# Two graph layers in one kernel: O^T of a batch moved to the end of a step, directly ahead of the next scores, and the sums of x1 blocks moved behind

## The chip, the cores and the metric

The kernel runs on one core of a Trainium2 chip. Its time is the device time of one execution in microseconds (us). Before the change three runs took 2452.73, 2454.88 and 2456.25 us, so the median is 2454.88 us. One more execution was recorded by the hardware profiler; its span is 2452.6 us, and every row of a profile below comes from such a profiled execution.

The engines are named as the profile names them: PE (TensorE, matrix products; PEld is its loading of weights), DVE (VectorE), ACT (ScalarE), POOL (GpSimd) and SP (the queue that issues most transfers).

## The reference, cut to what matters

The input is 128 batches of 128 tokens with 512 features, and a 128x128 adjacency matrix for each batch. Two layers follow each other, each with a residual and a layer norm:

```python
# layer 0: attention with 8 heads of 64 features
q, k, v = x @ Wq + bq, x @ Wk + bk, x @ Wv + bv
attn = softmax(where(adj > 0, q @ k.T / 8, -1e9))      # for each head
x1 = layernorm(x + relu((attn @ v) @ Wo + bo))
# layer 1: graph attention
Wh = x1 @ W
e = where(adj > 0, leaky(Wh @ a1 + (Wh @ a2).T), -9e15)
out = layernorm(x1 + leaky(softmax(e, axis=1) @ Wh))
```

All of it is in fp32. O^T is the transposed output of attention of one batch, (attn @ v)^T, 512 features by 128 tokens, and x1 is the output of layer 0.

## The kernel before, in words

The work is a software pipeline over the batches. One pass of the loop `for t in range(-3, END)` (line 929, END = 124) is called a step. The order of every engine's instructions is the order in which the code records them (`manual_schedule`, line 855), so where a line stands in a step is where it stands in each engine's queue. In a step t from 3 on, the following is under way at once:

- the softmax of batch t (class Softmax): `scores` (L506) on PE, mask and maxima on DVE (L520, L529), `exp` and `divide` on ACT (L540, L554), with the reciprocals on DVE (L550) between them; then `spread`, which writes the probabilities to DRAM and fetches them back in blocks (L560, L566);
- the end of attention of batch t - 1 (the variable `last`): `transpose` of the probabilities into paT on DVE (L575), `attend`, which computes O^T on PE (L588), and `copy`, which moves O^T with its bias from PSUM to the tile oT on ACT (L602);
- the projections q, k and v of the next group of four batches (`group_product`, L354), a product at a time wherever `group()` stands;
- the product of a pair of batches (`pair_product`, L435), a product at a time wherever `pair()` stands: layer 0's with Wo (class LayerZero) in odd steps, layer 1's with W (class LayerOne) in even steps;
- layer 1's attention of batch t - 7 (class Edge): `turn` on PE (L784, L785), `product` on PE (L818) with a copy to the tile z on ACT (L824), and its norm a step later (the variable `fin`): L828, L829 and L632 on DVE, L638 and L640 on POOL, L653 on DVE.

The large products use the Strassen-Winograd scheme: seven products of half-size blocks in place of eight, called p1 to p7, in the order of the table ORDER (line 272): p1, p5, p6, p2, p7, p4, p3. They need sums of blocks of the left operand, which POOL computes: xS from xT (sum_x), oS from oT (Softmax.sum) and x1S from x1T (LayerZero.sum), each with the four operations of `left_blocks` (L263 to L266). Inside one scheme, p1, p6, p7 and p4 add up in one PSUM bank, p_y; between them ACT copies out what the bank holds (t0, t2 and t3; L446 for a pair), and the next product into p_y waits for that copy.

Scores and O^T use TensorE in parts. For the scores each matmul contracts over 64 rows, and the two heads of a couple use the upper and the lower half of the array's rows (the profile writes 64*128). For O^T each matmul has 64 output columns, and the two heads use the left and right halves of the columns (128*64). All other products use the whole array (128*128).

PSUM tiles of one bank come from a ring of five (`ps_mm`, line 97): scores, p_y, p_w, p_x, p_e, p_oT and p_h take their turn in it in the order in which the code asks for them. The group's products have three banks of their own (st_y, st_w, st_x).

Before the change, in a step from t = 3 on, O^T of batch t - 1 stands after `sm.divide(6, 7)` and `mask_float`, between the fifth product of the pair (p7) and the fourth `group()` of the step. Its copy follows at once in even steps; in odd steps it stands after `pair(2)`. In even steps the sums oS of the pair that is then complete follow the copy. The sums x1S of layer 0's pair stand at the end of an even step, after the transposes of x1T (L233). In steps with t % 4 == 0, `sum_x` gives POOL the sums of a whole group after `fin.rstd`; they work on twice as many elements.

The step ends with `fin.product` (p_h) and `fin.copy`, and the next one begins with the scores. After the loop, the rest of the work is written out as a list of pieces (PLAN, line 1142).

Of the kernel before, what the change touches and what calls it, by code (L numbers as in the profile page):

```python
# [24 lines left out]
def kernel(  # L25
# [95 lines left out]
    def load_blocks(w, columns, queue, spread_rows=True, only=None):  # L121

        for o, t in enumerate(columns):
            if only not in (None, o):
                continue
            if spread_rows:
                rows = w.rearrange("(q k c i) (o f) -> o q i k c f", q=4, k=2, c=2, o=2)
                for q in range(4):
                    queue.dma_start(t[32 * q : 32 * q + 32, :, :, :HALF], rows[o, q])
            else:  # L130
                rows = w.rearrange("(k c p) (o f) -> o k p c f", k=2, c=2, o=2)
                for k in range(2):
                    queue.dma_start(t[:, k, :, :HALF], rows[o, k])
# [4 lines left out]
    def right_blocks(t):  # L138

        return [  # L140
            lambda: nc.vector.tensor_sub(t[2], t[2], t[0]),
            lambda: nc.vector.tensor_sub(t[5], t[3], t[2]),
            lambda: nc.vector.tensor_sub(t[4], t[5], t[0]),
            lambda: nc.vector.tensor_sub(t[6], t[1], t[5]),
        ]

    def places(w):
        return [w[:, n] for n in range(7)]

    def columns(w):  # L150
        return w[:, 0:2], w[:, 2:4]
# [23 lines left out]
    def load_bias():  # L175
        nc.sync.dma_start(bo_b, bo.partition_broadcast(P))
        return [lambda: nc.vector.tensor_sub(bo_b[:, HALF:], bo_b[:, HALF:], bo_b[:, :HALF])]

    def load_w1():

        load_blocks(W1, columns(w1), nc.sync)
        a_b = work.tile([P, 2, D], F32, name="a_b", tag="x1T")
        nc.sync.dma_start(
            a_b.rearrange("p s f -> p (s f)"),
            a1.rearrange("f o -> (f o)").partition_broadcast(P),
        )
        sums = small.tile([P, 2, 2, 2, 2], F32, name="wa", bufs=1)

        def dots(k, o, c):
            def run():  # L190
                for s in range(2):
                    scr = work.tile([P, HALF], F32, name="wa_scr", tag="x1S")
                    nc.vector.scalar_tensor_tensor(
                        scr,
                        w1[:, 2 * o + k, c, :HALF],
                        1.0,
                        a_b[:, s, o * HALF : (o + 1) * HALF],
                        op0=ALU.mult,
                        op1=ALU.mult,
                        accum_out=sums[:, s, k, o, c : c + 1],  # L200
                    )

            return run

        def last_column(k, o):
            def run():
                for c in range(2):
                    nc.vector.tensor_add(
                        w1[:, 2 * o + k, c, HALF:],
                        sums[:, o, k, 0, c : c + 1],  # L210
                        sums[:, o, k, 1, c : c + 1],
                    )

            return run

        every = [(k, o) for k in range(2) for o in range(2)]
        ops = [dots(k, o, c) for k, o in every for c in range(2)]
        return ops + [last_column(k, o) for k, o in every] + right_blocks(places(w1))
# [19 lines left out]
    def load_x(b):  # L238
        X[b] = spread(x[b])

    def load_residual(b):

        X1[b] = work.tile([P, D], F32, name="x1", bufs=7)
        nc.sync.dma_start(X1[b], x[b])
# [7 lines left out]
    def sum_x(g):  # L252
        sums = big.tile([P, 3, 2, 2 * P], F32, name="xS")
        XS[g], ops = left_blocks(XT[g], sums)
        return lambda: [op() for op in ops]
# [219 lines left out]
    def load_mask(b):  # L475
        MF[b] = small.tile([P, P], I32, name="adj", bufs=2)
        nc.sync.dma_start(MF[b], adj[b])

    def mask_float(b):
        a = MF[b]  # L480
        MF[b] = small.tile([P, P], BF16, name="mf", bufs=9)
        nc.scalar.copy(MF[b], a)
# [362 lines left out]
    def on(b):  # L845
        return 0 <= b < B
# [14 lines left out]
    none = Nothing()  # L861
    group_steps = []
    later = []
    zero = {}
    chores = []
    sm = fin = edge = none
# [61 lines left out]
    END = B - GROUP  # L928
    for t in range(-3, END):
        pair_steps = []  # L930
        if t % GROUP == 1 and on(t + 3):
            group_steps, v_pieces, fetch_v = products((t + 3) // GROUP)
        if t % 2 == 1 and on(t - 3):
            pair_steps = zero[(t - 3) // 2] = LayerZero((t - 3) // 2)
            pair_steps = pair_steps.steps()
        if t % 2 == 0 and on(t - 6):
            pair_steps = LayerOne((t - 6) // 2).steps()

        def group(n=1):
            for _ in range(min(n, len(group_steps))):  # L940
                group_steps.pop(0)()
            for _ in range(min(3 * n if t == -3 else n, len(chores))):
                chores.pop(0)()

        def pair(n=1):
            for _ in range(min(n, len(pair_steps))):
                pair_steps.pop(0)()

        if on(t + 1):
            load_mask(t + 1)  # L950
        if t == -1:
            load_blocks(Wo, columns(wo), nc.sync, spread_rows=False)
            late_chores = right_blocks(places(wo)) + load_bias()
        if t == 1:
            late_chores = load_w1()
        if t in (0, 2):
            chores += late_chores

        last, sm = sm, Softmax(t) if on(t) else none
        sm.scores()  # L960
        if t % 2 == 1 and on(t - 3):
            zero[(t - 3) // 2].by()
            zero[(t - 3) // 2].bw()
        while later:
            later.pop(0).go_back()
        if t < 3:
            sm.maxima()
            group(2)
            if on(t - 2):
                load_residual(t - 2)  # L970
            if t == 0 and on(GROUP):
                sum_x(1)()
            sm.exp(0, 1, 2, 3)
            last.transpose()
            group()
            sm.reciprocals(0)
            sm.exp(4, 5, 6, 7)
            sm.reciprocals(1)
            sm.divide(0, 1, 2)
            group()  # L980
            last.attend()
            sm.divide(3, 4)
            last.copy()
            if t % 2 == 0 and t > 0:
                last.sum(0, 1, 2, 3)
            sm.divide(5, 6, 7)
            if on(t + 1):
                mask_float(t + 1)
        else:
            sm.maxima()  # L990
            group()
            edge = Edge(t - 7) if on(t - 7) else none
            edge.turn()
            edge.add()
            fin.residual()
            if on(t - 2):
                load_residual(t - 2)
            edge.maxima()
            fin.stats()
            fin.rstd()  # L1000
            if t % GROUP == 0 and on(t + GROUP):
                sum_x(t // GROUP + 1)()
            pair()
            sm.exp(0, 1, 2, 3)
            edge.exp()
            pair()
            sm.exp(4, 5)
            last.transpose()
            group()
            sm.reciprocals(0)  # L1010
            pair()
            sm.exp(6)
            fin.apply()
            fin.store()
            sm.exp(7)
            edge.divide()
            pair()
            sm.reciprocals(1)
            sm.divide(0, 1, 2, 3)
            group()  # L1020
            sm.divide(4, 5)
            pair()
            sm.divide(6, 7)
            if on(t + 1):
                mask_float(t + 1)
            last.attend()
            if t % 2 == 0:
                last.copy()
                last.sum(0, 1, 2, 3)
            group()  # L1030
        sm.spread()
        for b in x_turns(t):
            transpose_x(b)
        for b in x_turns(t + 1):
            load_x(b)
        if on(t + 1):
            mask(t + 1)
        pair(2)
        if t % 2 == 1 and t >= 3:
            last.copy()  # L1040
        if t % 2 == 0 and on(t - 4):
            layer = zero.pop((t - 4) // 2)
            layer.transpose(0)
            layer.transpose(1)
            layer.sum(0, 1, 2, 3)
        group(21 if t % GROUP == 0 else 1)
        fin = edge
        fin.product()
        fin.copy()

# [180 lines left out]
```

## Time and profile before

| what | value |
|---|---|
| median of three runs | 2454.88 us |
| span of the profiled execution | 2452.6 us |
| one step, from one scores block to the next (1016.01 to 1034.28 us) | 18.27 us |
| O^T on PE (L588), 2016 matmuls | 138.8 us busy, mean 280 ns of one |
| scores on PE (L506), 2048 matmuls | 148.8 us busy, mean 285 ns of one |
| ACT idle ahead of the copies of O^T (L602) | 192.0 us |
| POOL, one sum of x1 blocks (L263 to L266) | 726 to 742 ns |
| DVE, z's norm applied (L653), mean of 116 | 696 ns |

Busy time counts an engine as busy while any of its instructions runs; the matmuls of a block overlap, so their mean duration is longer than their share of the busy time. In the chain of waits each piece has its start, the time that it adds to the chain, and what it is. In the timeline each row has the start, the duration of the merged instructions from the first start to the last end, and in brackets the idle time before them and what ended it.

### The profile page before, as it was taken

The page shows a single profiled execution, that of the slowest core. Times are in us where ns is not written, and L with a number is a line of the kernel's source. Part 1 is how long each engine was busy: PE and PEld are TensorE (multiplying, and loading weights), DVE is VectorE, ACT ScalarE, POOL GpSimd, SP SyncE. Part 2 cuts the span into 40 slices and gives each one's busy share as a digit, 9 for nine tenths or more (in the row PEclk, how much of TensorE's full clock was granted, in tenths as well). Part 3 has the DMA queues.
Part 4 walks back from the last instruction along what each step waited for, and adds up shares of the span by engine and source line. Part 5 has one row for each costly group of instructions (what it writes and reads, how often), then busy time and mean ns, then how long its engine had stood idle before and what let it go on. Part 6 is the DMA issues. An engine that isn't in the chain of part 4 may idle for free.

```text
span 2452.6 us, 43635 instructions
## 1 busy us (share of the span) xinstructions
PE 2412.3 (98%) x13585; PEld 1989.0 (81%) x13585; DVE 1802.0 (73%) x3731; ACT 1478.2 (60%) x5334; POOL 789.8 (32%) x1195
## 2 busy tenths in 40 slices
PE   8899999999999999999999999999999999999997
PEld 6688888888888888888888888888888888888874
DVE  5667777777777777777777777777777777777777
ACT  3566556556656665665666566656656665666574
POOL 2222323323233223233233332232332333322325
PEclk9999999999999999999999999999999999999999
DMA  6644544544545445445445454454454454544443
GB/s 190 179 148 142 166 149 152 169 146 148 167 147 166 154 141 168 145 154 169 149 146 171 146 163 157 140 168 146 152 171 146 146 171 145 164 152 149 149 157 105
DMA packets 351111, 379.91 MB, mean 155 GB/s; under 512 B 38936, under 2 KB 255008, under 8 KB 350880
## 3 DMA queue, kind: packets, MB, share of 16 engines
q1 hardware_dynamic: 350016, 376.07, 47.7%
q8 instruction: 109, 1.79, 0.3%
q10 hardware_dynamic: 864, 1.05, 0.2%
q14 instruction: 122, 1.00, 0.1%
HBM read 240.91 MB, written 136.05 MB: 154 GB/s over the span
## 4 chain that ended last, share of the span: by engine, by line
PE 93%; issue 1%; DMA 1%; DVE 1%; ACT 1%; POOL 1%; SPq 1%; DVEq 0%; POOLq 0%; ACTq 0%
PE st_y L354 27%; PE p_y L435 17%; PE st_w L354 14%; PE p_w L435 9%; PE st_x L354 7%; PE lg L506 5%; PE p_oT L588 5%; PE p_x L435 4%; PE p_h L818 4%; PE p_e L784 1%; DMA wv_n<-wv 0%; SPq L228 0%; ACT pa L540 0%; POOL rstd L640 0%; PE p_e L785 0%
## 5 line engine op out<-in xcount | busy, mean ns | idle before, releaser
L638 POOL TENSOR_SCALAR ve<-mv 128x1 f32<-128x1 f32 x256 | 69.1, 270 | 1323.7 <-DVE mv L634 1316.3
L540 ACT ACTIVATE pa<-pa,nmax 128x128 f32<-128x128 f32 x1008 | 392.4, 392 | 37.2 <-DVE nmax L529 32.7
L554 ACT ACTIVATE pa<-pa,rs 128x128 f32<-128x128 f32 x1008 | 331.5, 395 | 30.2 <-DVE rs L550 30.2
L602 ACT ACTIVATE oT<-p_oT,b_cols 128x128 f32<-128x128 f32 x504 | 142.9, 366 | 192.0 <-PE p_w L435 189.4
L520 DVE TENSOR_TENSOR pa<-lg,mf 128x512 f32<-128x512 f32 x252 | 161.8, 684 | 101.7 <-PE lg L506 96.5
L331 ACT COPY st_t<-st_y 128x512 f32<-128x512 f32 x192 | 110.5, 575 | 156.2 <-PE st_y L354 156.2
L506 PEld LDWEIGHTS lg<-kT,qT 64*128 64x128 f32 x2048 | 124.2, 187 | 92.3 <-issue 92.3
L540 ACT ACTIVATION_READ_ACCUMULATOR pa<-pa,nmax 128x1 f32 x1008 | 190.6, 189 | 0.0
L640 POOL TENSOR_TENSOR rstd<-ve,mhalf 128x1 f32<-128x1 f32 x256 | 176.2, 688 | 21.3
L446 ACT COPY pr_t<-p_y 128x257 f32<-128x257 f32 (+1 forms) x375 | 137.1, 366 | 59.9 <-PE p_y L435 59.8
L575 DVE STREAM_TRANSPOSE paT<-paz 128x1024 f32<-128x1024 f32 x126 | 156.9, 1245 | 3.6 <-DMA paz<-pa_dram 1.8
L529 DVE TENSOR_REDUCE nmax<-pa 128x8 f32<-128x1024 f32 x126 | 153.7, 1220 | 4.4
L506 PE MATMUL lg<-kT,qT 64*128 64x128 f32 x2048 | 148.8, 285 | 0.0
L588 PEld LDWEIGHTS p_oT<-paT,v 128*64 128x64 f32 x2016 | 108.2, 137 | 46.8 <-issue 39.9
L588 PE MATMUL p_oT<-paT,v 128*64 128x128 f32 x2016 | 138.8, 280 | 5.0 <-DVE paT L575 5.0
L335 ACT ACTIVATE st_t<-st_y,b_cols 128x256 f32<-128x256 f32 x192 | 80.6, 470 | 97.2 <-PE st_y L354 97.2
L759 DVE TENSOR_TENSOR wh<-p_w,pr_t 128x257 f32<-128x257 f32 x122 | 51.5, 423 | 112.4 <-PE p_w L435 65.4
L435 PE MATMUL p_y<-w,x1T 128*128 128x257 f32 x496 | 131.6, 388 | 1.6 <-ACT wk L446 1.5
L435 PE MATMUL p_y<-wo,oT 128*128 128x256 f32 x504 | 132.7, 386 | 0.2 <-ACT p_y L456 0.2
L435 PE MATMUL p_y<-wo,oS 128*128 128x256 f32 x504 | 129.4, 379 | 0.0
L354 PE MATMUL st_y<-wv_n,xS 128*128 128x256 f32 x512 | 124.1, 385 | 4.0 <-ACT pa L554 2.3
L435 PE MATMUL p_y<-w,x1S 128*128 128x257 f32 x496 | 128.0, 380 | 0.0
(200 smaller groups left out, 5926.3 us busy)
## 6 DMA issues: line engine op xcount, KB each, us to landing
pa_dram<-pa SPq DMA_DIRECT2D x126, 512.0 KB, 2.6
paz<-pa_dram SPq DMA_DIRECT2D x504, 128.0 KB, 2.6
wv_n<-wv SPq DMA_DIRECT2D x224, 256.0 KB, 2.9
x<-in_x_dram SPq DMA_DIRECT2D x128, 256.0 KB, 2.9
x_dram<-x SPq DMA_DIRECT2D x128, 256.0 KB, 2.1
xz<-x_dram SPq DMA_DIRECT2D x512, 64.0 KB, 2.0
xz<-in_x_dram SPq DMA_DIRECT2D x496, 64.0 KB, 2.1
out_dram<-z SPq DMA_DIRECT2D x120, 256.0 KB, 2.5
```

Of the source, the lines that this page charges most:

```text
L354: nc.tensor.matmul(p[:, m, :], lhs, rhs, start=start and m == 0 and kc == 0, stop=True, skip_group_check=True,)
L435: nc.tensor.matmul(p[:, :width], xs()[n][:, kc, :], w[:, PLACE[n], kc, :], start=start and kc == 0, stop=True, skip_group_check=True,)
L446: nc.scalar.copy(t[:, :width], p[:, :width])
L506: nc.tensor.matmul(self.lg[r][:, c, :], q[rows, c, cols], k[rows, c, cols], start=c == 0, stop=True, skip_group_check=True,)
L520: nc.vector.tensor_add(by_head[:, r * NC : (r + 1) * NC], self.lg[r].rearrange("p c (b k) -> p c b k", b=4), mf.unsqueeze(1).to_broadcast( ...
L529: nc.vector.tensor_reduce(self.nmax, by_head, AX.XY, ALU.max, negate=True)
L540: nc.scalar.activation(self.pa[:, :, h, :], self.pa[:, :, h, :], AF.Exp, bias=self.nmax[:, h : h + 1], accum_out=self.sums[:, h : h + 1],)
L554: nc.scalar.activation(self.pa[:, :, h, :], self.pa[:, :, h, :], AF.Copy, scale=self.rs[:, h : h + 1])
L575: nc.vector.transpose(self.paT.rearrange("p h (a i) -> p a h i", i=32), self.paz.rearrange("p a (h k) -> p a h k", k=32),)
L588: nc.tensor.matmul(self.oT[r * HD : (r + 1) * HD, c, :], v[:, h * HD : (h + 1) * HD], self.paT[:, r * NC + c, :], start=c == 0, stop=True, ...
L602: nc.scalar.activation(OT[pair][:, c, h * P : (h + 1) * P], self.oT[:, c, :], AF.Identity, bias=b_cols[:, 1, c : c + 1],)
L640: nc.gpsimd.tensor_tensor(self.r, ve, mhalf, ALU.pow)
```

## The change

O^T of batch t - 1 (`last.attend`) leaves its place in the middle of the step and goes to the end, after `fin.product` and `fin.copy`, so that the next instructions on PE are the scores of the next step. Its copy on ACT and the sums oS on POOL go with it. The sums of x1 blocks are no longer recorded at the end of an even step; they are kept in a list and recorded in the next step, after `fin.rstd`. This holds from t = 3 on; earlier steps and PLAN are as they were.

```diff
--- before.py
+++ after.py
@@ -861,6 +861,12 @@
     none = Nothing()
     group_steps = []
     later = []
+    sums = []
+
+    def x1_sums():
+        while sums:
+            sums.pop().sum(0, 1, 2, 3)
+
     zero = {}
     chores = []
     sm = fin = edge = none
@@ -998,6 +1004,7 @@
             edge.maxima()
             fin.stats()
             fin.rstd()
+            x1_sums()
             if t % GROUP == 0 and on(t + GROUP):
                 sum_x(t // GROUP + 1)()
             pair()
@@ -1023,10 +1030,6 @@
             sm.divide(6, 7)
             if on(t + 1):
                 mask_float(t + 1)
-            last.attend()
-            if t % 2 == 0:
-                last.copy()
-                last.sum(0, 1, 2, 3)
             group()
         sm.spread()
         for b in x_turns(t):
@@ -1036,17 +1039,23 @@
         if on(t + 1):
             mask(t + 1)
         pair(2)
-        if t % 2 == 1 and t >= 3:
-            last.copy()
         if t % 2 == 0 and on(t - 4):
             layer = zero.pop((t - 4) // 2)
             layer.transpose(0)
             layer.transpose(1)
-            layer.sum(0, 1, 2, 3)
+            sums.append(layer)
         group(21 if t % GROUP == 0 else 1)
         fin = edge
         fin.product()
         fin.copy()
+        if t >= 3:
+
+            last.attend()
+            last.copy()
+            if t % 2 == 0:
+                last.sum(0, 1, 2, 3)
+        if t == END - 1 or t < 3:
+            x1_sums()
 
 
 
```

## The prediction

> **What bounds the kernel now.** I read the page's busy table and slices first, then busy time by stretch, then the chain of waits inside one step, then the timeline.
>
> ```profile
> PE 2412.3 (98%) x13585; PEld 1989.0 (81%) x13585; DVE 1802.0 (73%) x3731; ACT 1478.2 (60%) x5334; POOL 789.8 (32%) x1195
> ...
> 130.00:200.00 70.00, 70.00 (x406) 58.47 (x405) 48.08 (x94) 41.01 (x153) 22.52 (x32) 1.00 0.50 155
> 200.00:1200.00 1000.00, 1000.00 (x5666) 828.10 (x5665) 741.05 (x1540) 611.47 (x2221) 318.97 (x478) 1.00 0.48 155
> 1200.00:2340.00 1140.00, 1139.60 (x6457) 943.41 (x6456) 843.38 (x1747) 695.58 (x2527) 367.64 (x548) 1.00 0.47 154
> ```
>
> The columns of the last three are the stretch, its length, then the busy time of PE, PEld, DVE, ACT, POOL. From 130 to 2340 us PE is idle for 0.4 us in all, at full clock. No other engine sets the time there: only shorter PE work or a new PE wait moves it. So I price the PE sequence. The chain over one even and one odd step's seam (start, length, what):
>
> ```profile
> 1024.43 1.73 PE st_y L354 x8
> 1026.16 0.86 PE p_y L435 x4
> 1027.02 1.02 PE p_oT L588 x16
> 1028.04 1.93 PE st_x L354 x8
> 1029.97 0.86 PE p_y L435 x4
> 1030.83 0.86 PE p_w L435 x4
> 1031.69 1.73 PE st_y L354 x8
> 1033.42 0.86 PE p_h L818 x2
> 1034.28 1.09 PE lg L506 x16
> 1035.37 1.92 PE st_y L354 x8
> ```
>
> Eight 128x256 matmuls take 1.73 us, but 1.92 or 1.93 when they follow an O^T block (p_oT) or a scores block (lg). Each visit to a tiled block therefore leaves 0.19 us with the full-size work after it: O^T costs 1.02 + 0.19 = 1.21, scores 1.09 + 0.19 = 1.28. (The weight loads' waits in "issue" ahead of lg and p_oT, 92.3 and 40.6 us, are the same seams seen from PEld.)
>
> **What the Trainium skill says.** "TensorEngine Tiling (Array Packing)", Tiling Modes, Key Properties: changing the tiling mode, not just the tile, drains TensorE. The trace agrees as far as it can: a fixed price at each seam. It gives no price, and doesn't say whether a change between two tiled modes costs as much as one from full size. "Advanced Engine Details and Errata", VectorE Performance Modes, Mode Summary: VectorE's second SBUF port is shared with GpSimd, so two-port Vector instructions and GpSimd instructions block each other. The trace agrees: L653 on z takes 0.51 us alone and 1.25 us beside POOL's xS sums, in the third listing.
>
> **Part 1: O^T directly ahead of the scores.** Per step, before: full, O^T, full, scores, full. After: full, O^T, scores, full, for t = 3 to 122 (the O^T of t = 123 is followed by a full product): 120 pairs. Same instructions, one pass through full size less. Is the seam between two tiled blocks as cheap as one seam? The trace has one such pair, in the tail, in the other order (scores, then O^T):
>
> ```profile
> 2365.72 1.03 PE L435 MATMUL p_y<-w,wq 128*128 128x257 f32 x4
> 2366.68 1.16 PE L506 MATMUL lg<-kT,qT 64*128 64x128 f32 x16
> 2367.78 1.09 PE L588 MATMUL p_oT<-paT,v 128*64 128x128 f32 x16
> 2368.80 0.32 PE L784 MATMUL p_e<-ident,wh 128*128 128x128 f32 x1
> ```
>
> From start to start: scores to O^T 1.10, as 1034.28 to 1035.37 above; O^T to the next 1.02. So O^T put beside scores cost 1.02 there, not 1.21: 0.19 saved. I take the same for the reverse order, an estimate from these rows. Ends: nothing saved (if the seam between the two modes costs as much as the pass through full size), or 0.36 (O^T at its bare streaming time: 8 concurrent pairs at half of the 0.216 of a 128x256, 0.86, so 1.21 - 0.86). 120 x 0.19 = **22.8 us off**.
>
> **Part 2: what O^T's old place hid.** O^T stood between product p7 of the running pair (with its ScalarE copy t3 of the bank p_y) and, one group product later, p4, which accumulates into p_y and must wait for that copy. The room from p7's end to p4 was O^T's 1.21 + 1.73 and is now 1.73. At t = 8, an even step with t % 4 == 0:
>
> ```profile
> 180.91 1.26 POOL L263 TENSOR_TENSOR xS<-xT 128x512 f32<-128x512 f32 x1
> 181.20 1.25 DVE L653 TENSOR_SCALAR z<-z,mv,rstd 128x512 f32<-128x512 f32 x1
> 182.56 1.11 DVE L813 TENSOR_SCALAR att<-att,rt 128x128 f32<-128x128 f32 x1
> 183.93 0.16 DVE L550 RECIPROCAL rs<-sums 128x4 f32<-128x4 f32 x1
> 184.12 0.69 ACT L554 ACTIVATE pa<-pa,rs 128x128 f32<-128x128 f32 x2 [0.98 <-DVE rs L550]
> 184.72 0.35 ACT L446 COPY pr_t<-p_y 128x257 f32<-128x257 f32 x1
> ```
>
> The group's xS sums on POOL slow two DVE operations, so the reciprocal is late, so ScalarE's divides, so the t3 copy, done at 185.07. p4 began at 186.20, 1.13 later; O^T gone, it could begin at 184.99, before the copy is done. A release takes about 0.05 us to reach PE (a copy done at 51.30, its matmul at 51.35), and a product whose weight load couldn't run ahead loses 0.10 more (eight take 1.83 instead of 1.73 after that wait): 0.08 + 0.05 + 0.10 = 0.23, say 0.25 us. The steps are t = 8, 12, ..., 120, 29 of them: 29 x 0.25 = **7.3 us on**. For t % 4 == 2 the copy leaves 1.36 us before p4 and so 0.15 after: at or just inside the release; nothing taken, up to 0.05 x 29 = 1.5 as the other end. For odd t it leaves 1.94 (t = 9) and 1.88 (t = 11), so 0.7: nothing.
>
> **Part 3: x1 sums into the next odd step.** Four POOL operations of 0.73 us leave the end of even steps and follow fin.rstd in odd ones; behind them in POOL's queue stand only the pair's rstd, asked for some 5 us later, and they are read a step later. But they now lie beside L653 on z and L813 on att. Placing them at t = 11 by the times of that step, z waits for the end of the second sum (0.51 becomes 0.9) and att for the third (0.29 becomes 0.5): the second reciprocal moves from 239.45 to 240.1. ScalarE was busy until 239.95 with a group copy, so the divides slip 0.2 and the room of 0.7 becomes 0.5. Nothing; at the other end both wait a whole operation, the copy is 0.9 late, and p4 waits 0.3 to 0.4 in the 29 steps t % 4 == 3: 12 us on. A gain at the even step's end (mask and x1T transposes free of POOL) lies on DVE, off the path: nothing.
>
> **Part 4: the O^T copies and sums at the step's end.** ScalarE copies O^T (4 at 0.31 us pitch) after z's copy, done some 2.4 us after O^T's start, and in odd steps then the two bias copies, 3.1. The first pair product p1 starts at 1.02 + 1.09 + 1.92 + 0.17 = 4.2, p5 0.9 later, needing bias and the first oS sum (2.4 + 0.8 = 3.2). Room above 1 us: nothing. Scores' banks: of the five in the ring, scores take the same as before (p_oT and p_h only change places). ScalarE's idle time of 189.4 us ahead of L602, waiting for p_w, goes elsewhere: off the path. SP's transfers keep their order; paT was ready long before; the tail's plan is untouched and shifts whole.
>
> **Sum.** -22.8 + 7.3 = -15.5 us on the profiled 2452.6, so 2437.1; against the median 2454.88 of three runs, **2439.4**.
>
> **Rivals.** (B) No new wait on p4, or the seam saves more: 2454.9 - 22.8 = 2432, down to 2428. For it: the copy misses by only 0.08 us. Against: the same 1.12 to 1.14 in nearly all of the 29. (C) More steps wait on the t3 copy, part 3's other end: 2439 + 1.5 + 12, up to 2452. For it: DVE loses about 0.7 us in every odd step. Against: ScalarE's group copy hides most. (D) The slower one: the seam from O^T's column tiles to the scores' row tiles costs a full pass, so nothing is saved and the p4 waits stay: 2454.9 + 7.3 = 2462. It decides above 0.17 us of extra price at that seam. For it: only the opposite order is in the trace, once. Against: that pair cost nothing extra. (E) The change fails to put them together: excluded; in the built order each of the 120 O^T blocks stands directly ahead of its scores.
>
> **How the numbers follow.** Chances: mine (2435 to 2443) 0.62, B 0.13, C 0.14, D 0.07, gains and losses that cancel 0.04. The range 2430 to 2448 leaves out D, the cancelling case and the ends of B and C. Within 0.2% (4.9 us) is about what a measurement can't tell from no change: faster 0.86, same 0.07, slower 0.07.
>
> **What would show it.** In the chain: p_oT 1.02, lg 1.09, then one 1.92, and 1.73 for the group product after p7; steps of 18.27 us become 18.08, those with t % 4 == 0 become 0.06 longer (-0.19 + 0.25). A new wait of PE for the copy at L446 in about 29 places of 0.1 us (0.35 for PEld); L653 on z rising from 696 to about 890 ns in the mean, L813 from 489 to about 600, with PE not noticing. If lg takes 1.2 or more after p_oT, part 1 is wrong; if PE waits on L446 in 58 or more places, part 3 is; if in none, part 2 is.

## The result, and the profile after

The changed kernel takes 2434.78 us (median of four runs, 2433.28 to 2438.01) against 2454.04 us for the kernel before; the ratio is 0.9922, with a 95% interval of 0.9905 to 0.994. In a later series it took 2437.68 against 2458.89 us, ratio 0.9913 (0.9898 to 0.9928). The profiled span falls from 2452.6 to 2431.4 us.

The page's busy table, and busy time by stretch (stretch, its length, then PE, PEld, DVE, ACT, POOL, granted clock, DMA share, GB/s), of the kernel after:

```profile
PE 2389.4 (98%) x13585; PEld 1997.9 (82%) x13585; DVE 1840.9 (76%) x3731; ACT 1488.7 (61%) x5334; POOL 805.8 (33%) x1195
...
200.00:1200.00 1000.00, 999.63 (x5722) 839.81 (x5721) 767.82 (x1553) 621.09 (x2241) 331.23 (x485) 1.00 0.49 157
1200.00:2320.00 1120.00, 1120.00 (x6402) 941.71 (x6401) 860.28 (x1740) 698.54 (x2522) 376.47 (x546) 1.00 0.48 155
```

PE is as full as before, with the same number of matmuls, and its busy time has fallen by 22.9 us: the work itself takes less time. DVE and POOL are busier by 38.9 and 16.0 us, and nothing follows from that. The chain of waits shows the seam (start, length, what):

```profile
1021.08 0.86 PE p_y L435 x4
1021.94 1.73 PE st_x L354 x8
1023.67 0.86 PE p_y L435 x4
1024.53 0.86 PE p_w L435 x4
1025.39 1.73 PE st_y L354 x8
1027.12 0.86 PE p_h L818 x2
1027.98 1.02 PE p_oT L588 x16
1029.00 1.09 PE lg L506 x16
1030.10 1.92 PE st_y L354 x8
```

The group product behind p7 takes 1.73 us where it took 1.93, and the scores still 1.09 although they follow O^T directly. The 120 seams between the two blocks can be compared start by start in the trace. From the last O^T matmul to the first of the scores it is 202 or 203 ns, from the last scores matmul to the full-size one behind it 202 as well, and before the change from the last O^T matmul to a full-size one 203. So a change from column tiles to row tiles costs what one change to the full array costs. What is saved is the rest of one visit: 93 ns on the way in (522 ns from the last matmul of p_h to the next block, where a 512-column matmul alone has 429) and 105 ns on the way out (the first full-size matmul has 320 or 321 ns to the next, the others 216). Together that is 0.198 us.

Every class of step gets shorter by just this. From one scores block to the next, worked out as medians from the starts in the two traces:

| t % 4 | before, us | after, us |
|---|---|---|
| 0 | 20.033 | 19.835 |
| 1 | 18.267 | 18.069 |
| 2 | 18.307 | 18.107 |
| 3 | 18.267 | 18.069 |

120 times 0.198 is 23.8 us. The span fell by 21.2, and the difference is a balance of four terms. Two were lost: the start (from the scores of t = 4 to those of t = 5 this execution takes 22.33 us instead of 18.02; up to the scores of t = 5 it has lost 4.3 us against what the seams give) and three steps (t = 20, 60 and 83 are longer than their class by 0.57, 0.33 and 0.11 us). Two were won without the change being shown to be their cause: a wait of 0.5 us at t = 76 that the profile of before has, and the tail, 2.2 us shorter than its seam explains. In the tail of before the granted clock was 0.57 from 2388 to 2392 us; in the profile of after it was 1.00 at the same pieces of work (2368 to 2372). The timeline at t = 4, before and after, and then the clock by stretch, before and after (busy columns as above):

```profile
109.51 1.09 PE L588 MATMUL p_oT<-paT,v 128*64 128x128 f32 x16 [0.62 <-DVE paT L575]
112.92 1.97 PE L354 MATMUL st_y<-wv_n,xS 128*128 128x256 f32 x8 [2.32 <-ACT pa L554]
```

```profile
106.92 1.99 PE L354 MATMUL st_x<-wv_n,xT 128*128 128x256 f32 x8 [0.94 <-DMA wv_n<-wv]
113.22 2.83 PE L354 MATMUL st_y<-wv_n,xS 128*128 128x256 f32 x8 [4.31 <-DMA wv_n<-wv]
116.73 3.78 PE L354 MATMUL st_y<-wv_n,xT 128*128 128x256 f32 x8 [0.68 <-ACT st_t L331]
```

```profile
112.00:116.00 4.00, 1.99 (x9) 1.46 (x9) 1.34 (x4) 3.92 (x14) 0.47 (x1) 1.00 0.86 314
116.00:120.00 4.00, 4.00 (x22) 3.31 (x24) 3.72 (x6) 1.17 (x3) 3.31 (x5) 1.00 0.56 153
```

```profile
112.00:116.00 4.00, 2.78 (x8) 1.86 (x8) 0.31 (x1) 1.44 (x6) 0.00 (x0) 0.77 0.97 367
116.00:120.00 4.00, 3.33 (x9) 2.65 (x9) 2.61 (x5) 0.59 (x1) 0.00 (x0) 0.50 0.48 133
```

At t = 4 the pipeline has no pair of layer 1 yet, and PE has too little to do. In the profile of before, O^T fell into this hole and split it (0.62 us idle ahead of O^T, 2.32 behind it). In the profile of after the hole is 4.31 us in one piece, and after it the granted clock is 0.77 and then 0.50, so that eight matmuls take 2.83 and 3.78 us instead of 2.0. Before, the same two stretches had the clock at 1.00.

These two profiles alone make the place of O^T look dearer than it is. The kernel with only the x1 sums moved (below) has O^T in its old place, and its profile shows the same fall of the clock, with a hole of 3.04 us:

```profile
108.74 1.09 PE L588 MATMUL p_oT<-paT,v 128*64 128x128 f32 x16
112.88 2.54 PE L354 MATMUL st_y<-wv_n,xS 128*128 128x256 f32 x8 [3.04 <-DMA wv_n<-wv]
```

```profile
112.00:116.00 4.00, 2.54 (x8) 1.63 (x8) 0.53 (x1) 3.24 (x12) 1.16 (x2) 0.77 0.90 334
116.00:120.00 4.00, 3.91 (x9) 3.19 (x10) 3.30 (x5) 0.13 (x2) 2.58 (x4) 0.50 0.58 160
```

Over all twelve profiles of this study the step from t = 4 to t = 5 takes 18.02 to 21.28 us (median 20.8) in the six in which this step has O^T in its old place, and 21.57 to 23.01 us (median 22.1) in the six with O^T at the seam. Before's 18.02 us is the lowest of the twelve, and its profile is the only one in which the clock did not fall there. By these medians about 1.3 of the 4.3 us go with O^T's place; the rest is the difference between two executions.

The copy on which part 2 of the prediction rested is not late. In the whole of 130 to 2320 us PE waits for it once, at t = 83 (in total, times, longest):

```profile
PEld p_y L435 <- ACT pr_t L446: 0.2, 1, 0.2
```

The timeline of t = 8, once before and once after:

```profile
172.66 0.52 DVE L653 TENSOR_SCALAR x<-x,mv,rstd 128x512 f32<-128x512 f32 x1
173.40 2.00 PE L354 MATMUL st_w<-wv_n,xS 128*128 128x256 f32 x8
173.92 0.55 DVE L653 TENSOR_SCALAR x<-x,mv,rstd 128x512 f32<-128x512 f32 x1 [0.74 <-POOL rstd L640]
174.38 1.28 DVE L520 TENSOR_TENSOR pa<-lg,mf 128x512 f32<-128x512 f32 x2
```

```profile
176.17 0.55 DVE L653 TENSOR_SCALAR x<-x,mv,rstd 128x512 f32<-128x512 f32 x1 [0.74 <-POOL rstd L640]
176.68 1.99 PE L354 MATMUL st_w<-wv_n,xS 128*128 128x256 f32 x8
176.78 1.29 DVE L520 TENSOR_TENSOR pa<-lg,mf 128x512 f32<-128x512 f32 x2
...
187.13 0.35 ACT L446 COPY pr_t<-p_y 128x257 f32<-128x257 f32 x1
...
188.25 1.03 PE L435 MATMUL p_y<-w,x1T 128*128 128x257 f32 x4
```

The row of PE at 173.40 and 176.68 is the first product behind the scores, so it marks their end. Before, the mask's addition (L520) began 0.98 us later, because DVE still had layer 0's norms to apply (L653 on x, two of them, the second waiting for POOL). After, O^T stands ahead of the scores, the applies run during O^T and the scores, and the addition begins 0.10 us after the scores. The whole softmax of the step moves forward by 0.9 us against PE, the t3 copy with it: it is done at 187.48 and p4 begins at 188.25, a room of 0.77 us. In the median of the class the addition begins 0.16 us after the scores instead of 1.01; at t % 4 == 2 some backlog stays, 0.56 us instead of 1.60.

### The profile page after: what moved, and what is told of

The parts are those of the page before. It is cut to its first block, busy times and chain, and to the rows that moved or that the text cites. A ratio compares the mean times of both kernels' runs of the same rounds, so it can differ in the third digit from the quotient of the medians.

```text
span 2431.4 us, 43517 instructions
## 1 busy us (share of the span) xinstructions
PE 2389.4 (98%) x13585; PEld 1997.9 (82%) x13585; DVE 1840.9 (76%) x3731; ACT 1488.7 (61%) x5334; POOL 805.8 (33%) x1195
## 3 DMA queue, kind: packets, MB, share of 16 engines
q10 hardware_dynamic: 864, 1.05, 0.2%
## 4 chain that ended last, share of the span: by engine, by line
PE 91%; DVE 2%; DMA 2%; issue 2%; ACT 2%; POOL 1%; SPq 1%; DVEq 0%; POOLq 0%; ACTq 0%
PE st_y L354 26%; PE p_y L435 17%; PE st_w L354 13%; PE p_w L435 9%; PE st_x L354 6%; PE lg L506 5%; PE p_oT L588 5%; PE p_x L435 4%; PE p_h L818 4%; DMA wv_n<-wv 1%; DMA pa_dram<-pa 1%; PE p_e L784 1%; ACT pa L554 1%; SPq L228 0%; ACT pa L540 0%
## 5 line engine op out<-in xcount | busy, mean ns | idle before, releaser
L520 DVE TENSOR_TENSOR pa<-lg,mf 128x512 f32<-128x512 f32 x252 | 162.0, 685 | 163.3 <-PE lg L506 158.0
L263 POOL TENSOR_TENSOR oS<-oT 128x256 f32<-128x256 f32 x63 | 45.8, 728 | 642.8 <-ACT oT L602 642.8
L446 ACT COPY pr_t<-p_y 128x257 f32<-128x257 f32 (+1 forms) x375 | 137.5, 367 | 48.7 <-PE p_y L435 48.7
```

What stands on the lines that cost most here:

```text
L446: nc.scalar.copy(t[:, :width], p[:, :width])
L520: nc.vector.tensor_add(by_head[:, r * NC : (r + 1) * NC], self.lg[r].rearrange("p c (b k) -> p c b k", b=4), mf.unsqueeze(1).to_broadcast( ...
```

## The experiments

The room below is always the time from the end of the t3 copy (L446) to the first matmul of p4, worked out from the rows of each trace as a median over the steps of one class.

**Is it the seam, or the late place?** Two kernels keep O^T at the seam of two steps. In the first p_h stands between O^T and the scores, in the second O^T follows the scores:

```diff
+        if t >= 3:
+            last.attend()
         fin.product()
         fin.copy()
         if t >= 3:
-            last.attend()
             last.copy()
```

> O^T at the end of the step as in the changed kernel, but ahead of p_h, so that p_h (two full-size matmuls) stands between O^T and the scores; x1 sums as in the changed kernel. Theory (the gain is one drained seam less per step): no gain from the seams, steps of 18.27 us as before, and the start's loss of about 4 us at t = 4 stays: about 2458 us, slower than before by 0.1 to 0.2%. Rival (the gain comes from the late place, which takes work out of the middle of the step): as fast as the changed kernel, about 2435 us, steps of 18.07 us.

```diff
         sm.scores()
...
+        held.attend()
+        held.copy()
+        if t % 2 == 1:
+            held.sum(0, 1, 2, 3)
...
         if t >= 3:
-            last.attend()
-            last.copy()
-            if t % 2 == 0:
-                last.sum(0, 1, 2, 3)
+            held = last
```

> O^T directly behind the next step's scores instead of directly ahead of them (scores, O^T, full). Theory (any pair of tiled blocks side by side saves one seam, 0.198 us a step, in either order): steps of 18.07 us, about 2435 us. Rival (the saving belongs to the order O^T, scores; or the pair products of an odd step wait for O^T's copies and sums, which now come some 1 us later against p1): 0.1 to 0.5 us more in odd steps, 2440 to 2460 us.

Measured: the first 2462.96 us, ratio 1.0029 (1.0019 to 1.004) to the kernel before; the second 2448.05 us, 0.9966 (0.9953 to 0.9979). The chain of waits, first kernel, then second:

```profile
1018.57 1.02 PE p_oT L588 x16
1019.59 1.05 PE p_h L818 x2
1020.65 1.09 PE lg L506 x16
1021.74 1.92 PE st_y L354 x8
```

```profile
1030.47 0.86 PE p_h L818 x2
1031.33 1.09 PE lg L506 x16
1032.42 1.02 PE p_oT L588 x16
1033.45 1.92 PE st_y L354 x8
```

Two full-size matmuls in between bring the price back at once: p_h takes 1.05 instead of 0.86, and the steps of three classes take what they took before the change (20.032, 18.267 and 18.304 us). So the late place alone gives nothing. In the second kernel the order is turned round and the steps are 18.069, 18.107 and 19.834 us in three classes, so the saving doesn't depend on the order. The steps with t % 4 == 3 are an exception in both: 18.440 and 18.313 us. There PE waits for the copy, in the waits from 130 to 2320 us (in total, times, longest), first kernel, then second:

```profile
PEld p_y L435 <- ACT pr_t L446: 9.1, 28, 0.7
```

```profile
PEld p_y L435 <- ACT pr_t L446: 11.0, 28, 0.7
```

This is the p4 wait of the prediction, of 0.17 and 0.24 us a step, in another class of step and from another cause. In these kernels O^T is copied later against the scores (at t % 4 == 3 the first oS sum starts 1.81 and 3.45 us after the start of the scores, in the changed kernel 1.34), so the oS sums on POOL lie beside DVE's work on z in this class, and there it takes longer: in the first kernel L828 takes 1.13 us instead of 0.68, in the second L828 takes 0.77 and L829 1.10 instead of 0.69. In the first kernel z's norm, the second reciprocal and the t3 copy all come 0.44 or 0.45 us later than in the changed kernel, which uses up its room of 0.43. No run of its own tests this cause; it is read from the traces. The rival in my expectation for the second kernel was another wait in odd steps, of the pair's products for O^T's copies and sums; that one did not come. Against the 2435 us of its theory the second kernel is 13 us slow: this wait is 7 us in 28 steps, and waits for blocks of wv (below) are 5 us in six steps. In the first kernel they are 5 and 3 us, enough for its 6.7 us above the kernel before.

**The two halves of the change apart.** O^T moved with the x1 sums left (`layer.sum(0, 1, 2, 3)` in place of `sums.append(layer)`), and the sums moved with O^T left:

> O^T moved as in the changed kernel, the x1 sums left at the end of even steps. Theory (the x1 move does nothing for the time): 2435 us within 0.2%, L653 and L813 back to 0.51 and 0.29 us in odd steps. Rival (the x1 move is needed: at the step's end the oS sums queue behind the x1 sums on POOL and p5 waits): new PE waits for POOL in odd steps, up to 0.5 us x 60, so up to 2465 us. A third: the DVE delays of the x1 move cost something in the changed kernel, then this is faster by 1 to 5 us.

> The x1 sums moved alone, O^T in its old place. Theory: no change, 2454 us within 0.2%, although L653 on z rises to about 0.96 us in odd steps. Rival: DVE's delay reaches the copy of p_y and PE waits: slower by 1 to 10 us.

Measured: 2434.86 us, ratio 0.9913 (0.9898 to 0.9928), and 2455.96 us, ratio 0.9999 (0.999 to 1.0007). The whole effect is O^T's. The x1 sums do what part 3 said: alone, they raise L653 on z beside them from 0.51 to 0.72 us at t % 4 == 1 and 0.93 at t % 4 == 3 (0.96 expected), lower the room at t % 4 == 3 from 1.88 to 1.66 us, and PE doesn't notice. The row of L653 on z, with O^T alone and with the sums alone (busy us, mean ns, idle before):

```profile
L653 DVE TENSOR_SCALAR z<-z,mv,rstd 128x512 f32<-128x512 f32 x116 | 80.8, 696 | 0.0
```

```profile
L653 DVE TENSOR_SCALAR z<-z,mv,rstd 128x512 f32<-128x512 f32 x116 | 98.5, 849 | 0.0
```

**Why the t3 copy was not late.** The kernel before, with layer 0's return (`go_back`) behind the maxima. The return is less than the recorded expectations take it for: it applies and stores the second of layer 0's two norms and fetches both batches. The first apply and its store are recorded in the odd step before and stay where they are, although DVE comes to that apply only in this step:

```diff
-        while later:
-            later.pop(0).go_back()
...
             sm.maxima()
+            while later:
+                later.pop(0).go_back()
             group()
```

> The kernel before with one edit: layer 0's return stands after the maxima instead of between the scores and the mask, so that DVE's two applies of the norm no longer stand ahead of the mask's addition. Theory (in even steps the t3 copy of the bank p_y was late because DVE had not finished these applies when the scores were done, so room for it does not shrink when O^T moves ahead of the scores): the first mask addition starts 0.1 us after the scores' end instead of 1.0, the room between the t3 copy and p4 at t % 4 == 0 grows from 1.13 to about 2.0 us, time unchanged (2454 us within 0.2%). Rival (the copy's lateness is set inside the step, by POOL's xS sums alone, as the prediction had it): the room stays at 1.13 us.

Measured: 2457.47 us in one run, beside 2455.55 to 2459.93 for the kernel before in the same series. The mask's addition begins 0.1 us after the scores at t % 4 == 0 instead of 1.01, and the room grows from 1.12 to 1.56 us, not to the 2.0 that I had expected and not staying where it was, as the rival had it. The one apply that the edit moves now stands behind the maxima and still ahead of z's norm, so z's apply comes 0.45 us earlier instead of 0.9 (7.38 us after the scores instead of 7.83), and the room gains 0.43. So the run shows that this backlog reaches the room, with half the size that was expected. The three kernels below that combine this return with O^T at the seam fit: z's apply comes 0.41 us later than in the changed kernel, and the room at t % 4 == 0 falls from 0.72 to 0.31 us. In the changed kernel z's apply comes at 6.98, 0.85 earlier; added to the -0.08 that the prediction had worked out for t = 8, that makes 0.77, and the trace has 0.77 there and 0.72 in the median. At t % 4 == 2 it is 1.04 earlier (8.42 to 7.38) and the room 1.15 instead of the 0.15 predicted.

**What O^T's old place did hide.** Four kernels, and the changed one again, look at t = 4 and at the blocks of wv. In the first, O^T moves from t = 5 on only. In the second, in addition, layer 0's return stands behind the first group product, so that SP issues a block of wv ahead of it. The other two follow below.

> The changed kernel again, for its spread and as the partner of the next two. Both theories: 2433 to 2438 us; the profile shows one wait above 4 us for a block of wv at t = 4 and a few small ones (0.1 to 0.6 us) in later steps with t % 4 == 0.

> As the changed kernel, but in steps 3 and 4, while the pipeline is still filling, O^T stays in its old place. Theory (at t = 4 O^T had filled part of a wait for a block of wv; without it PE idles 4.3 us, and the granted clock then falls for the next products): the 4.3 us lost between the scores of t = 4 and t = 5 come back, less two seams of 0.2: 2434.8 - 3.9 = 2431 us. Rival (the loss at t = 4 is a late transfer that comes with the new order anyhow): 2435 us, the wait stays, and the step from t = 4 to 5 takes 22.3 us again.

```diff
-        while later:
-            later.pop(0).go_back()
...
             sm.maxima()
             group()
+            while later:
+                later.pop(0).go_back()
```

> As the run before (O^T moved from t = 5 on), and layer 0's return (its norm applied, stored and fetched again: two stores and eight block transfers on SP's queue) stands after the maxima and the first group product of the step instead of straight after the scores, so that SP issues the block of wv for the step's fourth group product ahead of these ten. Theory (what O^T's old place still hid in later steps is the landing of that block, now 1.2 us nearer to its use): the small waits in steps with t % 4 == 0 go, 0.5 to 3 us faster than the run before, 2428 to 2431 us, with less spread. Rival (those waits are chance and not SP's order): no difference to the run before. Other rival: x1T's transposes at the step's end then wait for the later transfers, slower.

Measured, in one series: the changed kernel 2437.68 us (ratio 0.9913), from t = 5 on 2436.20 (0.9909, 0.9895 to 0.9924), with the earlier fetch 2433.92 (0.9897, 0.9881 to 0.9914). The changed kernel's second profile has more waits for wv than the first; from 130 to 2320 us:

```profile
PEld st_y L354 <- DMA wv_n<-wv: 6.6, 7, 1.3
PE st_y L354 <- DMA wv_n<-wv: 3.8, 6, 0.9
```

They fall into t = 20, 40, 60, 80, 96, 100 and 120, where the steps take 0.3 to 1.15 us more than their class. SP's rows and PE's at t = 20 of that run show what the product waits for (on SP the length is the issuing):

```profile
402.38 0.45 SPq L704 DMA_DIRECT2D x_dram<-x  x1
403.86 4.31 SPq L228 DMA_DIRECT2D xz<-x_dram  x8
...
408.27 0.38 SPq L395 DMA_DIRECT2D wv_n<-wv  x1
...
411.54 1.99 PE L354 MATMUL st_y<-wv_n,xS 128*128 128x256 f32 x8 [0.53 <-DMA wv_n<-wv]
```

The block of wv for the fourth group product is issued at 408.27, behind the store (402.38) and the eight block transfers of layer 0's return, and lands about 3 us later. Before the change the product came 1.1 us later (12.06 us after the scores' start instead of 10.94), and the block was there in all steps but t = 76. With the return behind the first group product this issue comes 3.12 us after the scores' start instead of 8.36 at t = 20, and no wait for wv above 0.12 us is left from 130 to 2320 us. The kernel of the experiment before this one, with the late return and O^T in its old place, shows the same from the other side: there the product stays at 12.06 and the issue is later (8.47 us after the scores' start in the median, 7.17 in the kernel before), and its trace has waits for wv in eight steps, 0.3 to 0.9 us each. So it is the distance from issue to use that counts. Over all steps of this class in the changed kernel's second profile the issue comes at 7.16 us in the median, and the block is in time; why it comes more than 1 us later in some steps is not shown.

With O^T moved from t = 5 on, the step from t = 4 to 5 fell from 22.70 to 19.94 us, by 2.8 of the 3.9 us expected, and the time missed the expected 2431 us: the steps up to t = 4 had taken 1.2 us longer, and the waits for wv were still there, so that the median fell by 1.5 us only. So I ran both edits for steps from t = 5 on only, and the earlier fetch alone from t = 3 on:

> Both edits for steps from t = 5 on only: O^T ahead of the scores, and layer 0's return behind the first group product; steps 3 and 4 as in the kernel before. Theory (two separate costs of the changed kernel: PE's wait and the clock's fall at t = 4, worth 3 to 4 us, and the late blocks of wv at t % 4 == 0, worth 1 to 6 us a run): the step from t = 4 to 5 takes at most 20 us as with the change from t = 5 on alone, the others 19.84 and 18.07: 2431 us, about 2 to 3 us below the next kernel. Rival (the start's time is set by the first loads, which vary by 1 to 2 us, and what is saved at t = 4 is not seen in the end): no difference to the next kernel, 2434 us.

> The changed kernel (O^T moved from t = 3 on) with layer 0's return behind the first group product in every step. Theory: no waits for wv in steps with t % 4 == 0 after the start, so mean steps of 19.84 there, but 22 us or more from t = 4 to 5: 2433 to 2435 us, 3 us faster than the changed kernel. Rival: the return's place has nothing to do with it, 2437 us.

Measured: 2431.80 us (ratio 0.9903, 0.9887 to 0.992) and 2431.37 us (0.9899, 0.9884 to 0.9913) against 2456.42 us. In the traces the waits for wv are gone in both: in the first, all steps from t = 8 to 122 lie within 0.05 us of their class, in the second one step is 0.08 us off. The step from t = 4 to 5 takes 21.03 us in the first, not the 20 expected at most, and 21.61 in the second, so the cure at t = 4 gave 0.6 us between these two profiles. In time there is no difference between them. The earlier fetch is worth about 3 us (0.9897 against 0.9909 for the kernel with O^T moved from t = 5 on, in one series; 0.9899 against 0.9913 for the changed kernel, in two; the intervals overlap, and it is the traces that show the waits gone). Whether the cure at t = 4 is worth anything stays open: the first 80 us, which wait for the first loads, differ by up to 5 us between the profiled runs here (the scores of t = 3 begin between 82.0 and 86.9 us), more than what is to be seen. These two kernels and the one before them have the lowest ratios of the study, below both the kernel before and the changed one.

## Why the prediction was right or wrong

The forecast was 2439.4 us, 2430 to 2448, and faster with 0.86. Measured: 2434.78 us, faster; the gain was 19.3 us by the medians and 21.2 between the profiles where the sum had 15.5. That the number came so near is in part luck: the sum's second term (7.3 us on) did not come at all, and losses that the sum did not have, at the start and in waits for wv, took its place.

- Part 1 was right in kind and size: 0.19 us a pair was forecast, 0.198 measured, 22.8 and 23.8 us for 120. The one pair of the tail in the other order was a fair witness: its seam had 202 ns, as the 120 have. The sentence of the Trainium skill in "TensorEngine Tiling (Array Packing)", Tiling Modes, Key Properties, that a change of mode drains TensorE, agrees with all of it: 202 ns at each change. Measured here in addition: two tiled modes side by side cost one seam less than two visits from the full array.
- Part 2 is the step that failed. "29 x 0.25 = 7.3 us on" measured nothing: PE waited for the copy once, 0.2 us. The term compared the copy with p4 as if both started from the scores, took the copy's lateness to be set by POOL's xS sums within the step, and took O^T out of p4's way only. But in even steps the softmax started from DVE's backlog of the step before, and O^T went into the wait for that backlog: the room taken ahead of p4 was given back ahead of the scores, as far as DVE used it. The trace of before showed it, in 1.01 and 1.60 us from the scores to the mask's addition at t % 4 == 0 and 2, against 0.10 in odd steps. (The row with L653 at 1.25 us, for which the prediction points to its third listing, stands in its fourth.)
- What did take some of the gain was not in the sum. At t = 4 it was 4.3 us between the first two profiles (PE's idle time there grew by 1.4, and at the lower clock the three products behind the hole took 8.85 us instead of 5.86), of which about 1.3 go with O^T's place by the medians of twelve profiles. Waits for wv lengthened steps by 1 us in the first profile and some 6 in the second. The prediction had passed over both with "SP's transfers keep their order". They do; the product that uses them came nearer.
- Part 3 held: z's apply went to 851 ns in the mean (890 forecast), att to 626 (600), the room at t % 4 == 3 to 0.43 us instead of the 0.5, and PE waited in one such step only (t = 83, the 0.2 us above). Part 4 held too, with one thing missed: the oS sums now lie beside L828 and L829 (724 and 760 ns instead of 682 and 692), without effect here, but just that made PE wait in the two kernels with O^T placed otherwise.
- Rival B, no wait on p4, came nearest to what happened, for a reason that it did not give. D is excluded by the 120 seams; C's wait came only in the two kernels above.

## What to carry to other kernels

Where TensorE is full, put blocks in different tile modes side by side: here each visit from the full array paid the same price at its edges, for O^T and for the scores, and two visits made one saved 0.198 us. When a block of work moves in a full queue, ask of each other queue not only what waits behind it but from where its chain starts: a chain that starts from a backlog gets back ahead of the block's new place what it loses at the old one. And compare the first steps over several profiles before a loss there is laid to the change. Look, too, at whatever lands just in time for the work that now comes earlier, and at the pipeline's start, where the same block may have been filling a hole.

## What the runs showed of the hardware that was not expected

- A hole on PE can bring the granted clock down for some microseconds after it, and the length of the hole alone does not say by how much. At t = 4 a hole of 4.31 us brought it to 0.77 and then 0.50 in the next two stretches of 4 us (after), one of 3.04 us to the same 0.77 and 0.50 (x1 sums alone), and one of 2.80 us to 0.55 and 0.60 (both edits from t = 5 on). One of 3.18 us cost half of that, 0.90 and 0.81 in stretches of 6 us (O^T moved from t = 5 on), and holes of 0.62 and 2.32 us left it at 1.00 (before). The Trainium skill, "TensorE: Matmul & The Clock Gate", Part 1: The HAM clock gate, says that the clock is halved after at least one idle window of about 3.4 us. The trace agrees on the half; but here single holes of 2.80 and 3.04 us were followed by it too, and the measurement decides.
- A POOL operation on 128x256 or 128x512 elements holds up a DVE operation that reads two SBUF tensors, not only the two-port ones: L829 (z and x1 from SBUF) takes 692 ns alone and 1100 where an oS sum is still under way; L653 on z takes 514 alone, and 720 to 930 beside the x1 sums. POOL is held up as well: in the changed kernel its last oS sum takes 1.28 us where L828 begins 0.02 us after it (t = 61) and 0.73 where L828 comes 0.6 us later (t = 63). The mask's addition and layer 1's additions (L759), with one operand in PSUM, keep their 686 and 426 ns beside POOL's sums. The Trainium skill, "GPSIMD Engine Reference", Key points, names both kinds of DVE instructions as those that contend with GpSimd for SBUF; the trace agrees.
